# A graph-attention kernel with a new opening order, the elu minimum on another engine, and statistics combined in halves

## The chip, the core and the metric

The kernel runs on one NeuronCore of one Trainium2 chip. The core has five engines that run side by side, each with its own queue of instructions that it takes strictly in order: TensorE (PE in the profile, with its weight loads shown as PEld), VectorE (DVE), ScalarE (ACT), GpSimd (POOL) and SyncE (SP, which here only starts transfers). An instruction waits until the semaphores it names have been raised by other engines or by transfers; while it waits, everything behind it on the same engine waits too. The metric is the device time of one execution in microseconds. Before the change it is 2589.18 us, the median of three runs (2588.01 to 2589.99).

## The reference, cut to what matters

The input `x` has 16 graphs of 1024 nodes with 256 features; `adj` is one 1024 x 1024 adjacency matrix for all of them. Four layers follow each other. Each normalises, takes the positive part, runs a graph attention and adds the result to `x`:

```
h = maximum(layernorm(x), 0)
q = h @ W                                  # 256 -> 256, as H heads of D = 256 / H
e[i, j] = leaky(a_src . q[i] + a_dst . q[j])
w = softmax over j of e, only where adj[i, j] is set
x = x + elu(w @ q)                         # the last layer has relu in place of elu
```

Layers 0 and 2 have four heads of 64 columns, layers 1 and 3 one head of 256. All arithmetic is fp32.

## The kernel before, in words

**Steps.** A step is one layer of one graph, so there are 16 x 4 = 64 steps. `order_of_steps` interleaves four graphs (four "streams"), so that one-head and four-head steps alternate: the heads of the 64 steps run 4 4 4 1 4 1 1 4 1 4 1 ... 4 1 4 1 4 4 1 1 1. The two stretches in which four-head steps follow each other are the very beginning and shortly before the end.

**One step.** It has a preparation, a stretch of attention weights with aggregation, and a finish.
- Preparation (`preparation`, a list of 21 pieces). `stats` (DVE, L234) makes the layer norm's batch statistics of 4 of the 8 row blocks at a time; `combine` and `combine_end` (L257 to L269) turn them into a scale and a shift per row, in ten small instructions on GpSimd, for all eight blocks at once. `normalise` (ACT, L275) applies them, four instructions for each half of the rows; `transpose` (PE, L283) turns the half, eight instructions, and ACT moves the result out of PSUM with the positive part (L284). `project` multiplies by W (PE, L294), ACT moves each of eight results out (L296), and GpSimd scales them (L306). `factors`, `rows` and `fetch` send one attention factor per node through DRAM to all partitions.
- Weights (`weights`, DVE, L347): one instruction makes the 128 x 1024 attention weights of one head and one block of source nodes. A four-head step has 32 of them, a one-head step 8. They live in a pool of 18 buffers (`WBUFS`).
- Aggregation (`aggregate`, PE, L363): 8 groups of matmuls a step; ACT moves each group's result out of PSUM (L378). PSUM has four buffers for this ("bank") that transposes, projections and aggregations share.
- Finish (`finish`): divide by the softmax's sum (L395, and L405 on GpSimd), elu as `max(exp(min(y, 0)) - 1, y)`, and the addition to `x` (L418 on GpSimd). The minimum is on DVE in four-head steps (L404, done together with the division) and on GpSimd in one-head steps (L407); the exponential is on ACT (L411), the rest of elu on DVE (L417).

**The order of the work.** It is written out by the kernel's own planner, not by a scheduler. The main loop runs over the steps and their 8 groups; after group k of step n it emits the pieces of finish due at k and the pieces of preparations due at 8n + k (`agenda_of`, from tables such as `ONE` for one-head and `FOUR` for four-head steps: the entries are in groups, counted from two steps ahead). Then it emits the next weights, as far as buffers allow. So each engine's queue is fixed when the program is built.

**The opening.** Ahead of the loop the 8 blocks of the adjacency matrix are loaded, reduced to 0 or 1 on DVE (`sign`, L190), turned on PE (`turn`, L204), and stored as two masks, one by DVE (`positive`, L207) and one by ACT (`nonzero`, L211). Layer 0's weight columns are made (`columns`), and step 0 is prepared. Step 1 is prepared after that, step 2's statistics are emitted after step 0's first 8 weights, and the graphs of streams 2 and 3 are loaded (`load(i)`, L566) only once step 1 is prepared.

Of the kernel before, what the change touches and what calls it, by code (L numbers as in the profile page):

```python
# [38 lines left out]
STREAMS = 4  # L39
# [4 lines left out]

FOUR = (-8, -8, -5, -3, -2, -1, -1, 0, 0, 0, 0, 0, 0, 2, 2, 2, 2, 3, 8, 8, 10)
SHORT = (-4, -4, -4, -2, -2, -1, -1, 0, 0, 0, 0, 0, 0, 2, 2, 2, 2, 3, 8, 8, 10)
ONE = (2, 2, 2, 4, 4, 5, 5, 6, 6, 6, 6, 6, 6, 8, 8, 8, 8, 8, 10, 10, 12)
SOON = (0, 0, 0, 1, 2, 3, 3, 4, 4, 5, 5, 5, 5, 6, 6, 7, 7, 8, 9, 9, 11)  # L50
FIRST = (-2, -2, -2, -1, -1, -1, -1, -1, -1, -1, -1, -1, -1, -1, -1, -1, -1, -1, -1, -1, 3)
LATE = (0, 0, 0, 1, 1, 2, 2, 3, 3, 3, 3, 3, 3, 4, 4, 4, 4, 5, 6, 6, 8)


# [9 lines left out]
def kernel(ctx: ExitStack, tc: tile.TileContext, x, adj, ws, avs, out):  # L64
    nc = tc.nc
    B, N, F = x.shape
    C = N // P
# [61 lines left out]
    def weight_columns(l):  # L129

        H, slope, hs, _ = LAYERS[l]
        D = F // H
        st = {}

        def vectors(queue=nc.sync):

            st["a"] = prep.tile([P, HALF, H, D], F32, name="e")
            queue.dma_start(
                out=st["a"][0:1, 2:4],
                in_=bass.AP(tensor=avs[l].tensor, offset=avs[l].offset,  # L140
                            ap=[[0, 1], [D, 2], [hs, H], [1, D]]))

        def spread():
            pa = bank(2, H, D)
            nc.tensor.matmul(pa.rearrange("p t h d -> p (t h d)"), lhsT=ones[0:1, :],
                             rhs=st["a"][0:1, 2:4].rearrange("p t h d -> p (t h d)"),
                             start=True, stop=True)
            nc.scalar.activation(st["a"][:, 0:2], pa, AF.Copy)

        def columns():  # L150
            for k in range(K):
                for part in range(2):
                    prod = st["a"][:, 2 + part]
                    wk = heads_of(wx[l], H)[:, k]
                    nc.vector.tensor_mul(prod, wk[:, :, 0:D], st["a"][:, part])
                    nc.vector.tensor_reduce(
                        wk[:, :, D] if part else wx[l][:, k, F + H:F + 2 * H], prod, AX.X, ALU.add)
            st["sq"] = small.tile([P, K, H], F32, name="sq", bufs=1)
            wd = heads_of(wx[l], H)[:, :, :, D]
            nc.vector.tensor_tensor(st["sq"], wd, wd, op=ALU.mult)  # L160

        def bound():

            pn = bank(H)
            for k in range(K):
                nc.tensor.matmul(pn, lhsT=ones, rhs=st["sq"][:, k, :], start=(k == 0),
                                 stop=(k == K - 1))
            top = small.tile([P, 1], F32, name="top", bufs=1)
            nc.vector.tensor_reduce(top, pn, AX.X, ALU.max)
            nc.gpsimd.tensor_tensor(top, top, half1, op=ALU.pow)  # L170
            nc.gpsimd.tensor_scalar(cbias[l], top, 16.01, None, op0=ALU.mult)
            nc.gpsimd.tensor_scalar(nbias[l], top, -16.01 * slope, None, op0=ALU.mult)
            nc.gpsimd.tensor_scalar(rbias[l], top, -16.01 * (1.0 - slope), SHIFT,
                                    op0=ALU.mult, op1=ALU.add)

        return vectors, spread, columns, bound
# [45 lines left out]
    def preparation(n):  # L222
# [6 lines left out]
        def stats(half):  # L229
            if half == 0:  # L230
                st["bn"] = small.tile([P, C, 6], F32, name="bn")
            bn = st["bn"]
            for c in range(half * HALF, (half + 1) * HALF):
                nc.vector.bn_stats(bn[:, c, :], xs[b][:, c, :])  # L234
            if n == 0:
                q = slice(half * HALF, (half + 1) * HALF)
                if half == 1:
                    combine_end(slice(0, HALF), nc.vector)
                combine(q, nc.vector)
                if half == 1:  # L240
                    combine_end(q, nc.vector)

        def combine_all():
            if n > 0:
                combine(slice(0, C), nc.gpsimd)
                combine_end(slice(0, C), nc.gpsimd)

# [18 lines left out]
        def combine_end(q, engine):  # L266
            rstd, shift = (st[i][:, q] for i in ("rstd", "shift"))
            engine.tensor_tensor(shift, shift, rstd, op=ALU.mult)
            engine.tensor_scalar(shift, shift, -0.5, None, op0=ALU.mult)  # L269
# [110 lines left out]
    def finish(n):  # L380

        b, l = steps[n]
        H = LAYERS[l][0]
        D = F // H
        st = state[n]

        def views(half):
            s = slice(half * HALF, (half + 1) * HALF)
            return (xs[b][:, s, :].rearrange("p c (h d) -> p (c h) d", h=H),
                    st["y"][:, s, :, 0:D].rearrange("p c h d -> p (c h) d"),  # L390
                    st["r"][:, s, :].rearrange("p c h -> p (c h)"))

        def divide():
            st["r"] = small.tile([P, C, H], F32, name="r")
            nc.vector.reciprocal(st["r"], st["y"][:, :, :, D])  # L395

        def scaled(half):
            xh, yh, r = views(half)
            rb = r[:, :, None].to_broadcast([P, HALF * H, D])
            if l < L - 1:  # L400

                e = st["e", half] = prep.tile([P, HALF * H, D], F32, name="e")
                if H > 1:
                    nc.vector.scalar_tensor_tensor(e, yh, 0.0, rb, op0=ALU.min, op1=ALU.mult)  # L404
            nc.gpsimd.tensor_tensor(yh, yh, rb, op=ALU.mult)  # L405
            if l < L - 1 and H == 1:
                nc.gpsimd.tensor_scalar(e, yh, 0.0, -3.0e38, op0=ALU.min, op1=ALU.max)  # L407

        def exponential(half):
            if l < L - 1:  # L410
                nc.scalar.activation(st["e", half], st["e", half], AF.Exp)  # L411

        def add(half):
            xh, yh, r = views(half)
            if l < L - 1:
                e = st["e", half]
                nc.vector.scalar_tensor_tensor(e, e, -1.0, yh, op0=ALU.add, op1=ALU.max)  # L417
                nc.gpsimd.tensor_add(xh, xh, e)  # L418
                return
            nc.vector.scalar_tensor_tensor(xh, yh, 0.0, xh, op0=ALU.max, op1=ALU.add)  # L420

        def store(half):
            nc.sync.dma_start(
                out=out[b].rearrange("(p c) f -> p c f", p=P)[:, half * HALF:(half + 1) * HALF],
                in_=xs[b][:, half * HALF:(half + 1) * HALF, :])
            if half == 1 and b + STREAMS < B:
                load(b + STREAMS)


        at = (0, 0, 0, 0, 1, 1, 1) if H > 1 else (0, 0, 1, 1, 2, 2, 3)  # L430
        return list(zip(at, (divide, lambda: scaled(0), lambda: scaled(1), lambda: exponential(0),
                             lambda: exponential(1), lambda: add(0), lambda: add(1)))) + (
                    [(4, lambda: store(0)), (4, lambda: store(1))] if l == L - 1 else [])
# [60 lines left out]
    for n, (b, l) in enumerate(steps):  # L494

        free = 8 * (last[b % STREAMS] + 1) + (8 if l == 0 else 2) if b % STREAMS in last else -99
        last[b % STREAMS] = n
        start = 8 * (n - 2)
        kind = ONE if LAYERS[l][0] == 1 else SOON if n < 5 else FOUR
        if kind is FOUR and free > start + kind[0]:  # L500
            kind = SHORT
        if free > start + kind[0]:
# [10 lines left out]
    with tc.manual_schedule():  # L513
# [6 lines left out]
            blocks[c][0]()  # L520
        load(1)
        load_weights(1)
        nc.scalar.activation(warm, half1, AF.Exp)
        nc.vector.tensor_copy(identb, ident)
        layer[0][1]()
        first = [piece for _, piece in preparation(0)]

        def sign(c):

            if c < C:  # L530
                blocks[c][1]()
                blocks[c][2]()
            if c > 0:
                blocks[c - 1][3]()

        for i in (0, 1, 3, 4):
            first[i]()
        layer[0][2]()
        first[5]()
        first[6]()  # L540
        layer[0][3]()
        sign(0)
        for i, c in ((7, 1), (9, 2), (11, 3), (13, 4), (15, 5)):
            first[i]()
            first[i + 1]()
            sign(c)
        for piece in first[17:]:
            piece()
        for c in (4, 5, 0, 1, 2, 3):
            blocks[c][4]()  # L550
        done["prepared"] = 1
        plan(1)
        planned = 2
        prepare(-2)
        sign(6)
        sign(7)
        sign(8)
        emit_tiles(C, must=True)
        for _ in range(2):
            agenda.pop(0)[2]()  # L560
        blocks[6][4]()
        blocks[7][4]()
        prepare(-1)
        for i in range(2, STREAMS):
            load_weights(i)
            load(i)  # L566

        for l, at in ((1, 1), (2, 8 * 3 + 3), (3, 8 * 5 + 3)):
            for i, piece in zip((0, 1, 2, 8), layer[l]):
# [57 lines left out]
```

## Time and profile before

| what | number |
|---|---|
| time, median of three | 2589.18 us |
| span of the profiled execution | 2586.6 us |
| PE busy | 2508.0 us, 97% |
| DVE busy | 2024.0 us, 78% |
| ACT busy | 1129.3 us, 44% |
| GpSimd busy | 1034.3 us, 40% |
| mean granted TensorE clock | 0.992 |

The page also has the span cut into 40 slices of 64.7 us: PE is at 60% in the first, 80% in the second and 90% or more after that. A busy PE is not a PE at its peak: 256 aggregating matmul records of a four-head step take 7.69 us when nothing holds them up, and count as busy for longer when they arrive one weight buffer at a time. So the page's shares say where to look, and the timeline of a stretch says what ends each wait.

### The profile page before, as it was taken

What the parts mean: (1) busy time and instruction counts of PE and PEld (TensorE: products, weight loads), DVE (VectorE), ACT (ScalarE), POOL (GpSimd) and SP (SyncE); (2) the same over time, 40 slices, a digit from 0 to 9 for tenths busy, and PEclk for the clock granted to TensorE, in tenths of its full rate; (3) what the DMA queues carried; (4) which work ended last, traced back from release to release, by engine and by line L of the source; (5) the groups of instructions that cost most, each with busy time, mean ns of one, the idle gap of its engine ahead of it and who ended that gap; (6) DMA issues with size and microseconds to landing.
All of it is one profiled execution on the core that took longest, in us unless ns stands there. A gap on an engine that the chain in (4) does not pass through costs nothing.

```text
span 2586.6 us, 87821 instructions
## 1 busy us (share of the span) xinstructions
PE 2508.0 (97%) x40088; PEld 2257.8 (87%) x40088; DVE 2024.0 (78%) x2144; ACT 1129.3 (44%) x2502; POOL 1034.3 (40%) x1040
## 2 busy tenths in 40 slices
PE   6889999999999999999999999999999999999999
PEld 4788888899888899888899888998888998889888
DVE  5997678877778877778877778877778877787973
ACT  5344444434444444544344544344444345444341
POOL 2143444432443444543323444543433345444331
PEclk8899999999999999999999999999999999999999
DMA  3210011111112100102211111101112201111101
GB/s 142 73 44 35 18 34 43 43 60 59 59 51 76 43 27 27 43 35 75 76 53 66 43 35 43 43 19 68 50 59 76 76 11 43 35 43 43 52 18 57
DMA packets 36987, 128.98 MB, mean 50 GB/s; under 512 B 6278, under 2 KB 9094, under 8 KB 34696
## 3 DMA queue, kind: packets, MB, share of 16 engines
q1 hardware_dynamic: 36606, 123.36, 13.6%
q8 instruction: 314, 5.14, 0.8%
q14 instruction: 57, 0.47, 0.1%
q10 hardware_dynamic: 10, 0.00, 0.0%
HBM read 105.91 MB, written 17.43 MB: 48 GB/s over the span
## 4 chain that ended last, share of the span: by engine, by line
PE 57%; DVE 26%; POOL 9%; issue 5%; ACT 3%; DMA 1%; DVEq 0%; SPq 0%; ACTq 0%
PE bank L363 36%; DVE w L347 17%; PE bank L294 17%; POOL x L418 5%; PE bank L283 4%; DVE bn L234 3%; DVE e L417 2%; ACT xn L275 2%; DVE e L404 2%; POOL rstd L263 2%; DMA x<-in_x 0%; ACT e L411 0%; PE bank L318 0%; DVE r L395 0%; POOL shift L269 0%
## 5 line engine op out<-in xcount | busy, mean ns | idle before, releaser
L363 PE MATMUL bank<-whx,w 128*64 128x65 f32 x36864 | 1904.8, 241 | 32.6 <-DVE w L347 20.8
L363 PEld LDWEIGHTS bank<-whx,w 128*64 128x64 f32 x36864 | 1742.1, 144 | 176.5 <-DVE w L347 25.5
L347 DVE SCALAR_TENSOR_TENSOR w<-g,rcol,mask 128x1024 f32<-128x1024 f32 x1280 | 1540.4, 1273 | 378.0 <-PE bank L363 337.3
L378 ACT ACTIVATE y<-bank 128x260 f32<-128x260 f32 (+1 forms) x504 | 194.4, 386 | 1093.4 <-PE bank L363 1093.4
L306 POOL TENSOR_TENSOR whx<-whx 128x1024 f32<-128x1024 f32 x128 | 258.5, 2020 | 666.0 <-ACT whx L304 666.0
L405 POOL TENSOR_TENSOR y<-y,r 128x1024 f32<-128x1024 f32 x126 | 264.4, 2108 | 582.1 <-DVE e L404 454.9
L294 PE MATMUL bank<-wx,hT 128*128 128x264 f32 (+1 forms) x2048 | 476.5, 387 | 3.7 <-ACT hT L284 3.7
L294 PEld LDWEIGHTS bank<-wx,hT 128*128 128x128 f32 x2048 | 384.6, 191 | 66.3 <-ACT hT L284 4.6
L418 POOL TENSOR_TENSOR x<-x,e 128x1024 f32<-128x1024 f32 x96 | 248.0, 2593 | 135.7 <-DVE e L417 135.7
L275 ACT ACTIVATE xn<-x,shift,rstd 128x256 f32<-128x256 f32 x512 | 261.2, 590 | 82.9 <-POOL shift L269 80.8
L296 ACT ACTIVATE whx<-bank 128x264 f32<-128x264 f32 (+1 forms) x512 | 194.9, 386 | 208.1 <-PE bank L294 207.7
L234 DVE BATCH_NORM_STATS2 bn<-x 128x6 f32<-128x256 f32 x512 | 175.9, 412 | 97.2 <-POOL x L418 74.0
L417 DVE SCALAR_TENSOR_TENSOR e<-e,y 128x1024 f32<-128x1024 f32 x96 | 158.0, 1663 | 34.2 <-ACT e L411 26.9
L283 PE MATMUL bank<-ident,xn 128*128 128x128 f32 x1024 | 155.2, 281 | 22.9 <-ACT xn L275 22.4
L283 PEld LDWEIGHTS bank<-ident,xn 128*128 128x128 f32 x1024 | 120.4, 141 | 59.6 <-ACT xn L275 48.5
L342 ACT ACTIVATE g<-gs 128x1024 f32<-128x1024 f32 x160 | 163.6, 1022 | 11.1 <-DVE w L347 8.4
L284 ACT ACTIVATE hT<-bank 128x512 f32<-128x512 f32 x256 | 136.6, 585 | 0.3 <-PE bank L283 0.2
L263 POOL TENSOR_TENSOR rstd<-rstd,neghalf 128x8 f32<-128x8 f32 (+1 forms) x65 | 107.0, 1646 | 12.5 <-DVE shift L264 7.6
L411 ACT ACTIVATE e<-e 128x1024 f32<-128x1024 f32 x96 | 100.7, 1049 | 12.7 <-DVE e L404 12.7
L404 DVE SCALAR_TENSOR_TENSOR e<-y,r 128x1024 f32<-128x1024 f32 x64 | 75.6, 1222 | 2.5 <-DVE r L395 0.5
L420 DVE SCALAR_TENSOR_TENSOR x<-y,x 128x1024 f32<-128x1024 f32 x30 | 43.4, 1445 | 10.0 <-POOL y L405 10.0
L257 POOL TENSOR_TENSOR dev<-bn 128x8 f32<-128x8 f32 x63 | 14.6, 231 | 87.4 <-DVE bn L234 87.4
(63 smaller groups left out, 401.7 us busy)
## 6 DMA issues: line engine op xcount, KB each, us to landing
gs<-grow SPq DMA_DIRECT2D x160, 512.0 KB
x<-in_x SPq DMA_DIRECT2D x15, 1024.0 KB
out<-x SPq DMA_DIRECT2D x30, 512.0 KB
w<-in_adj SPq DMA_DIRECT2D x8, 512.0 KB
x<-in_x SPq DMA_DIRECT2D x2, 512.0 KB
wx<-in_L_gnn_W SPq DMA_DIRECT2D x8, 128.0 KB
out<-x SPq DMA_DIRECT2D x8, 128.0 KB
grow<-gT SPq DMA_DIRECT2D x32, 16.0 KB
```

The lines of the kernel that those rows point to most:

```text
L234: nc.vector.bn_stats(bn[:, c, :], xs[b][:, c, :])
L275: nc.scalar.activation(xn[:, q, :], xs[b][:, c, :], AF.Identity, bias=st["shift"][:, c:c + 1], scale=st["rstd"][:, c:c + 1])
L283: nc.tensor.transpose(pt[:, q, :], st["xn", half][:, q, k * P:(k + 1) * P], ident)
L294: nc.tensor.matmul(pw, lhsT=st["hT", half][:, k, q * P:(q + 1) * P], rhs=wx[l][:, k, :], start=(k == 0), stop=(k == K - 1))
L296: nc.scalar.activation(st["whx"][:, c, :], pw, AF.Copy)
L306: nc.gpsimd.tensor_tensor(wh[:, :, :, 0:D], wh[:, :, :, 0:D], wh[:, :, :, D:D + 1].to_broadcast([P, HALF, H, D]), op=ALU.mult)
L347: nc.vector.scalar_tensor_tensor(w, state[n]["g", h], state[n]["rcol"][:, jc, h:h + 1], masks[LAYERS[steps[n][1]][3]][:, jc, :], op0=ALU.m ...
L363: nc.tensor.matmul(acc[o % P:o % P + cols, q, :], lhsT=st["w", h, jc][:, o:o + cols], rhs=st["whx"][:, jc, h * (D + 1):(h + 1) * (D + 1)], ...
L378: nc.scalar.activation(st["y"][:, i0:i0 + per, h, :], acc, AF.Copy)
L405: nc.gpsimd.tensor_tensor(yh, yh, rb, op=ALU.mult)
L417: nc.vector.scalar_tensor_tensor(e, e, -1.0, yh, op0=ALU.add, op1=ALU.max)
L418: nc.gpsimd.tensor_add(xh, xh, e)
```

## The change

There are four edits.
1. **The opening** is written as one explicit list. Streams 2 and 3 (`load(2)`, `load(3)`) are loaded at the start, behind the adjacency matrix. Step 1's statistics move between the masks (`prepare(-4)`), and its two halves are normalised, turned and projected among step 0's first groups of aggregation instead of ahead of them (the new table `FIRST`). The two masks are made block by block as the turns arrive. Step 3's preparation is due one group later.
2. **The elu minimum** is placed by the step that runs beside it: on DVE where the next step has one head, on GpSimd where the next has four. Of the 64 steps this changes four: steps 0, 1 and 59 (from DVE to GpSimd) and step 5 (from GpSimd to DVE).
3. **Statistics in two parts**: in one-head steps the ten small GpSimd instructions run for each half of the row blocks, behind that half's statistics, instead of once for all eight blocks. Each half is normalised with its own result. Four-head steps keep the single combination.
4. **The last two steps** get a table of their own (`TIGHT`), which puts their preparations three groups later up to the transposes, and one to two groups later at the end.

The diff, without the lines that only move blank space:

```diff
-FIRST = (-2, -2, -2, -1, -1, -1, -1, -1, -1, -1, -1, -1, -1, -1, -1, -1, -1, -1, -1, -1, 3)
+FIRST = (-4, -4, -4, -2, 0, -1, -1, -1, -1, -1, -1, 1, 1, 2, 2, 2, 2, 2, 3, 3, 5)
+TIGHT = (5, 5, 5, 7, 7, 8, 8, 9, 9, 9, 9, 9, 9, 10, 10, 10, 10, 10, 11, 11, 13)
...
-        def columns():
-            for k in range(K):
+        def columns(ks=range(K)):
+            for k in ks:
...
+            q = slice(half * HALF, (half + 1) * HALF)
             if n == 0:
-                q = slice(half * HALF, (half + 1) * HALF)
                 if half == 1:
                     combine_end(slice(0, HALF), nc.vector)
                 combine(q, nc.vector)
-                if half == 1:
-                    combine_end(q, nc.vector)
+            elif H == 1:
+                combine(q, nc.gpsimd)
+                combine_end(q, nc.gpsimd)

         def combine_all():
-            if n > 0:
+            if n == 0:
+                combine_end(slice(HALF, C), nc.vector)
+            elif H > 1:
                 combine(slice(0, C), nc.gpsimd)
                 combine_end(slice(0, C), nc.gpsimd)
...
         def scaled(half):
+            time = LAYERS[steps[n + 1][1]][0] == 1
             if l < L - 1:
                 e = st["e", half] = prep.tile([P, HALF * H, D], F32, name="e")
-                if H > 1:
+                if time:
                     nc.vector.scalar_tensor_tensor(e, yh, 0.0, rb, op0=ALU.min, op1=ALU.mult)
             nc.gpsimd.tensor_tensor(yh, yh, rb, op=ALU.mult)
-            if l < L - 1 and H == 1:
+            if l < L - 1 and not time:
                 nc.gpsimd.tensor_scalar(e, yh, 0.0, -3.0e38, op0=ALU.min, op1=ALU.max)
...
-        start = 8 * (n - 2)
-        kind = ONE if LAYERS[l][0] == 1 else SOON if n < 5 else FOUR
+        start = 8 * (n - 2) + (n == 3)
+        kind = (ONE if n < len(steps) - 2 else TIGHT) if LAYERS[l][0] == 1 else SOON if n < 5 else FOUR
...
         load(1)
         load_weights(1)
+        for i in range(2, STREAMS):
+            load(i)
...
+        order = (
+            [first[0], first[1], first[3], lambda: layer[0][2](range(1)), first[2],
+             lambda: layer[0][2](range(1, K)), first[5], first[6], first[4], layer[0][3]]
+            + [blocks[c][1] for c in range(4)]
+            + [first[7], first[8], blocks[0][2], blocks[4][1], blocks[5][1], blocks[0][3],
+               first[9], first[10], blocks[1][2], blocks[0][4], blocks[6][1], blocks[7][1],
+               blocks[1][3], first[11], first[12], blocks[2][2], blocks[1][4],
+               lambda: prepare(-4), first[13], first[14], blocks[3][2], blocks[2][4],
+               blocks[2][3], blocks[3][3], first[15], first[16]]
+            + [first[17], blocks[4][2], blocks[5][2], first[18], first[19],
+               blocks[4][3], blocks[3][4], blocks[4][4], blocks[5][3], blocks[5][4],
+               blocks[6][2], blocks[7][2], blocks[6][3], blocks[6][4], blocks[7][3], blocks[7][4]])
         plan(1)
         planned = 2
+        for piece in order:
+            piece()
+        done["prepared"] = 1
+        emit_tiles(C // 2, must=True)
         prepare(-2)
-        sign(6)
-        sign(7)
-        sign(8)
         emit_tiles(C, must=True)
-        for _ in range(2):
-            agenda.pop(0)[2]()
-        blocks[6][4]()
-        blocks[7][4]()
         prepare(-1)
         for i in range(2, STREAMS):
             load_weights(i)
-            load(i)
```

More of the change, by code (lines that the diff above doesn't have):

```diff
@@ L157, in columns @@
                         wk[:, :, D] if part else wx[l][:, k, F + H:F + 2 * H], prod, AX.X, ALU.add)
+            if K - 1 not in ks:
+                return
             st["sq"] = small.tile([P, K, H], F32, name="sq", bufs=1)
@@ L526 @@
         first = [piece for _, piece in preparation(0)]
[L528 to L551, printed above, removed]
+        order = (
[10 more added lines that the diff above has]
+               blocks[6][2], blocks[7][2], blocks[6][3], blocks[6][4], blocks[7][3], blocks[7][4]])
         plan(1)
         planned = 2
+        for piece in order:
+            piece()
+        done["prepared"] = 1
+        emit_tiles(C // 2, must=True)
         prepare(-2)
-        sign(6)
-        sign(7)
-        sign(8)
         emit_tiles(C, must=True)
-        for _ in range(2):
-            agenda.pop(0)[2]()
-        blocks[6][4]()
-        blocks[7][4]()
         prepare(-1)
```

## The prediction

> **What bounds the kernel now.** I read the page's engine shares first, then the slices, then the waits, and last the timelines of the opening, of one step in the middle, and of the end.
>
> ```profile
> PE 2508.0 (97%) x40088; PEld 2257.8 (87%) x40088; DVE 2024.0 (78%) x2144; ACT 1129.3 (44%) x2502; POOL 1034.3 (40%) x1040
> ...
> PE   6889999999999999999999999999999999999999
> PEld 4788888899888899888899888998888998889888
> DVE  5997678877778877778877778877778877787973
> ```
>
> TensorE is the engine to keep fed. The first two slices (129 us) are the only ones in which it is plainly not, and there DVE is half idle in slice one and full in slices two and three. So the kernel has two regimes: an opening bound by DVE up to about 200 us, and then TensorE. What TensorE or DVE waits for:
>
> ```profile
> DVE bn L234 <- DMA x<-in_x: 23.3, 2, 20.0
> ...
> PE bank L283 <- ACT xn L275: 22.4, 87, 3.8
> ```
>
> The first line is one wait of 20.0 us on a load of `x`; the second is 87 small waits of the transposes for normalised rows, some 15 us of them outside the opening. They are the two places I price.
>
> ```profile
> 39.53 9.63 DVE L347 SCALAR_TENSOR_TENSOR w<-g,rcol,mask 128x1024 f32<-128x1024 f32 x8 [0.79 <-ACT g L342]
> 69.13 2.71 DVE L234 BATCH_NORM_STATS2 bn<-x 128x6 f32<-128x256 f32 x8 [19.98 <-DMA x<-in_x]
> 71.76 21.52 DVE L347 SCALAR_TENSOR_TENSOR w<-g,rcol,mask 128x1024 f32<-128x1024 f32 x18
> ```
>
> In the opening DVE makes 8 weights, then sits in front of step 2's statistics, whose graph was asked for only at 63.71 us and landed at 69 us. All later weights are queued behind. From 71.76 to 200 us DVE never idles for over 1 us.
>
> ```profile
> 888.54 5.58 POOL L418 TENSOR_TENSOR x<-x,e 128x1024 f32<-128x1024 f32 x2 [1.16 <-DVE e L417]
> ...
> 895.64 0.21 POOL L257 TENSOR_TENSOR dev<-bn 128x8 f32<-128x8 f32 x1 [1.52 <-DVE bn L234]
> ...
> 899.59 0.24 POOL L269 TENSOR_SCALAR shift<-shift 128x8 f32<-128x8 f32 x1
> ...
> 899.86 4.04 ACT L275 ACTIVATE xn<-x,shift,rstd 128x256 f32<-128x256 f32 x8 [2.26 <-POOL shift L269]
> ...
> 900.51 0.33 PE L283 MATMUL bank<-ident,xn 128*128 128x128 f32 x1
> 901.00 0.33 PE L283 MATMUL bank<-ident,xn 128*128 128x128 f32 x1 [0.16 <-ACT xn L275]
> ...
> 902.59 3.64 PE L363 MATMUL bank<-whx,w 128*128 128x257 f32 x16
> ```
>
> This is step 20, a one-head step in the middle. The ten small GpSimd instructions end at 899.83, ACT starts normalising at once, and the transposes follow ACT at one normalised block per 0.49 us. The eight transposes hold PE from 900.51 to 902.59, 2.08 us; unhindered they take 0.97 us (1381.79 to the next group at 1382.76). The loss is 1.1 us, more than the 0.49 us shown as idle, because the busy time is stretched too.
>
> **The Trainium skill.** "Perfetto Trace Analysis", section "Optimizing Scalar/DVE Operations", says that where ScalarE and VectorE aren't saturated but cause bubbles elsewhere, breaking up instructions may let work complete sooner: that is edit 3, and the trace agrees on the bubbles (GpSimd is 40% busy). The same section warns that moving work between DVE and GpSimd might not help, since they share an SBUF read port. "SBUF — State Buffer" names DVE instructions with two SBUF inputs as those that contend with GpSimd's reads. Here L417, which has two, takes 1.22 us alone and 1.66 us in the mean, 2.9 us at worst beside GpSimd, which agrees. "DMA: Bandwidth & Descriptors", section "Bandwidth", has 341 GB/s for a 1 MB load; the opening here moved 397 to 415 GB/s from 10 to 20 us.
>
> **Opening.** The two early loads (2 MB) at the 415 GB/s seen take 5.1 us. Transfers are idle from about 20 to 34 us, so they land by 26 us, hidden beside the mask work, ahead of the broadcasts. The first weight should stay near 39.5 us: the list holds the same 8 signs, 8 positives and 8 statistics on DVE, and the chain through step 0's projections to the broadcast of its factors is not shorter by more than a microsecond. Then 8 weights (9.6 us) and 8 statistics (2.7 us) end at 51.9 us, so DVE reaches weight 9 at 51.9 instead of 71.76: **19.9 us** earlier. TensorE must keep up. It starts aggregating near 48 instead of 60.35 us. From 60.35 us to the end of step 2 (209.81) it now does 3 steps of 1024 records at 7.69 us per 256 (92.3), three preparations of some 10 (30) and 2.5 of odds, 125 us in 149; the change adds half of step 1's preparation (5), so the earliest end is 48 + 130 = 178 us, and 20 us is within reach but tight. Following both queues, DVE would fill its 18 buffers once, some 4 us before TensorE ends step 0 at about 100 us: minus 4. The minimum: step 1 saves two L404 (2.4 us) and waits 0.2 to 0.8 us longer for the exponential. In step 0 only two weights lie between division and L417, and GpSimd's chain per half is 2.0 (L405) + 1.04 (L407) with 1.05 on ACT, ready at 4.1 and 7.2 us: two waits of 1.7 us take back the 2.4 saved. Behind that exponential on ACT are the moves out of PSUM, for which PE already waits 2.96 us at 172.7; that grows by 1.8 us where DVE is the bound anyway. Sum **19.9 - 4 + 2 = 18 us**; bounds 8 (TensorE binds earlier) and 22. From step 3 on both kernels are TensorE-bound, so it is kept.
>
> **Statistics in halves.** In the changed kernel's instruction order, everything from step 7 to 57 is the same on PE, DVE and ACT; only GpSimd differs. For all eight blocks the ten instructions take 4.19 us (895.64 to 899.83). No row shows nine of them at four blocks on GpSimd; the tenth, the power, takes 1.03 at four blocks in step 0 against 1.67. Bounds for a half: 3.5 us (the others as long as now, which their 0.29 us spacing suggests) and 4.2. I take 3.5. Half 0 can start when L418 ends, at 894.12, and is ready at 897.6, when ACT has just moved out a group (897.22 + 0.39). Four normalisations take 2.07: done at 899.7, before PE arrives at 900.5. The transposes then take 0.97: 1.1 us saved. Half 1 is ready at 901.1 (now 899.83), normalised at 903.2; ACT behind it moves out the waiting group and the transposes (0.3 + 1.06): 904.6. PE wants them at 901.4 + 3.5 = 904.9, so the new wait just fits, by 0.3 us. With 4.2 a half, half 1 comes at 902.5, ACT ends at 906.0, and a new wait of 1.1 us eats the gain. Of the 25 one-head steps from 8 to 56, 16 show 0.41 to 0.49 us of idle (1.1 lost), 8 show 0.71 to 0.81 (1.45 lost, by the same count at 1446.50), one 0.16 (0.4): 17.6 + 11.6 + 0.4 = 29.6 us. As the margin of 0.3 us won't hold always I take off 0.2 a step: **24 us**; bounds 0 and 30.
>
> **End.** Steps 59 and 60 are DVE-bound; the last weight of step 60 is done at 2474.8 and PE has no gap after it. The moved minimum of step 59 brings that some 1.4 us forward. The later preparation of step 62 moves 1 us of transposes behind it, and step 63's weights come one group (3.5 us) later, ending near 2558.7 where its first group would be done at 2558.2: 1 us. Sum 0, bounds -3 and +3. Step 5's minimum and step 3's shift lie beside TensorE-bound work: 0.
>
> **Forecast and rivals.**
> - Forecast, 0.62: 2589 - 18 - 24 = 2547 us.
> - The second half comes late and takes the whole gain of the halves (0.17): 2589 - 18 = 2571. For it: margin 0.3 us, GpSimd's unmeasured small instructions. Against: their spacing doesn't follow size.
> - TensorE binds the opening, which gives 8 (0.13): 2589 - 8 - 24 = 2557. For it: 130 us of its work in that stretch; against: it idles 13 us between 60 and 81 us, before DVE has caught up.
> - Slower (0.06): GpSimd's extra 2.8 us also delays the next four-head step's combination (now done at 903.92, wanted by ACT at 905.02), ACT stands in front of its moves, PE runs out of banks and loses 1.6 us in 25 steps, 40 us: 2589 - 18 + 40 = 2611. Against: that combination would end at 905.1, 0.1 late.
> - No change needs both gains to cancel: 0.02.
>
> Faster is the sum of the first three, 0.92. The range runs from all bounds at their best (2589 - 22 - 30 - 3 = 2534, and two for rounding), to the second rival and some microseconds (2574).
>
> **What would show it.** The wait of DVE on `x` of 20.0 us is gone and weight 9 starts near 52 us; step 2 ends near 192 us. In the middle the transposes' wait for normalised rows falls from 22.4 us to some 5, and a pair of steps takes 76.7 instead of 77.6 us. I am wrong if PE waits for the moved-out transposes (L284) in every one-head step, or if step 2 ends after 200 us.

## The result, and the profile after

The changed kernel takes 2560.54 us (median of four, 2558.53 to 2563.94), against 2588.6 us before: ratio 0.9894, 95% interval 0.9877 to 0.9911. It gains 28 us where 42 were forecast. Lines moved down by about eight: the weights are now L355, the aggregation L371, the move out of PSUM behind it L386, the transposes L291, normalising L283.

The page of the changed kernel, engine shares and slices:

```profile
PE 2497.2 (98%) x40088; PEld 2258.7 (88%) x40088; DVE 2018.9 (79%) x2140; ACT 1130.0 (44%) x2502; POOL 1110.1 (43%) x1364
...
PE   6899999999999999999999999999999999999899
...
DVE  8888578888778888778888778888778878778863
```

Slice three of PE went from 8 to 9 (before, three slices were below 90%, and not only the two that the texts above name), but slice 38, near the end, fell from 9 to 8. DVE is fuller in slice one (8 for 5). GpSimd has 324 more instructions and 76 us more busy time. Its waits (what waits, for what: us in total, times, longest):

```profile
DVE w L355 <- ACT g L350: 77.8, 9, 22.2
...
PE bank L291 <- ACT xn L283: 10.3, 4, 6.9
...
PE bank L371 <- ACT whx L304: 7.5, 2, 4.8
...
PE bank L326 <- ACT gcol L321: 7.1, 2, 6.3
...
PE bank L302 <- ACT y L386: 4.4, 9, 0.5
...
DVE bn L238 <- DMA x<-in_x: 3.3, 1, 3.3
```

The two waits that were priced are gone: DVE's 20.0 us on `x` (the 3.3 us left were there before, at the start), and the transposes' waits outside the opening, 0.4 us where there were 15.5; the other 9.9 of the 10.3 us lie in the opening. In their place stand waits that no sum had: one of 6.3 us of PE on ACT's `gcol` (L321, the factors that `rows` sends out), one of 4.8 us on ACT's move of a projection (L304; 2.96 us before), nine of 0.5 us on ACT's move of an aggregation (L386), and DVE's wait for `g` (the factors broadcast to all partitions), which went from 40.8 to 77.8 us, 37.5 of them for the weights of the last two steps.

The move out of PSUM of a step's eighth group (L386, on ACT) marks the end of that step, and in the last step, which has no such move, DVE's last reciprocal of a result does (L380). Differences between these marks in the trace divide the span into stages:

| stage (us) | before | after | gain | forecast |
|---|---|---|---|---|
| start to the end of step 2 | 209.81 | 199.42 | 10.4 | 18 |
| steps 3 to 7 | 201.6 | 201.6 | 0 | 0 |
| steps 8 to 58 | 1985.98 | 1962.25 | 23.7 | 24 |
| steps 59 to 63 | 185.09 | 192.37 | -7.3 | 0 |

Together 26.8 us, the difference of the two spans (2586.6 and 2559.7). The same kernel profiled a second time, as an experiment below, gives 196.93 for the opening, 1962.72 for the middle and 192.28 for the end. So the middle came as forecast, the opening brought 10 to 13 us of 18, and the end lost time where the sum had zero.

**The middle.** The same step 20 that the prediction read, now in the changed kernel (start and length in us):

```profile
878.04 0.19 POOL L265 TENSOR_TENSOR dev<-bn 128x4 f32<-128x4 f32 x1
...
881.32 0.23 POOL L277 TENSOR_SCALAR shift<-shift 128x4 f32<-128x4 f32 x1
...
881.59 2.08 ACT L283 ACTIVATE xn<-x,shift,rstd 128x256 f32<-128x256 f32 x4
...
884.55 1.03 PE L291 MATMUL bank<-ident,xn 128*128 128x128 f32 x8
884.79 0.23 POOL L277 TENSOR_SCALAR shift<-shift 128x4 f32<-128x4 f32 x1
...
885.05 2.07 ACT L283 ACTIVATE xn<-x,shift,rstd 128x256 f32<-128x256 f32 x4 [1.39 <-POOL shift L277]
...
887.30 1.06 ACT L292 ACTIVATE hT<-bank 128x512 f32<-128x512 f32 x2
```

A half takes 3.51 us on GpSimd (878.04 to 881.55), the 3.5 that the prediction took. Half 0 is normalised 0.9 us before the transposes begin, and they take 1.03 us without a break instead of 2.08. Half 1 is ready at 885.02; the moves behind it end at 888.36, and PE begins the projection that needs them at 888.90, with no wait: a margin of 0.5 us. Most one-head steps take 33.63 or 34.10 us where they took 34.56 or 35.02. The nine new waits of 0.5 us lie in steps of 34.10 us. At 660.54 us, for instance, GpSimd has combined the next four-head step's statistics 1.3 us later in the step than before, ACT normalises for that step first, from 658.14 to 660.21 us, and only then moves an aggregation out (L386, 660.12 us), for which PE's projection waits 0.49 us.

### The profile page after: what moved, and what is told of

Read it like the earlier page. It is cut to its first block, busy times and chain, and to the rows that moved or that the text cites. A ratio compares the mean times of both kernels' runs of the same rounds, so it can differ in the third digit from the quotient of the medians.

```text
span 2559.7 us, 88174 instructions
## 1 busy us (share of the span) xinstructions
PE 2497.2 (98%) x40088; PEld 2258.7 (88%) x40088; DVE 2018.9 (79%) x2140; ACT 1130.0 (44%) x2502; POOL 1110.1 (43%) x1364
## 3 DMA queue, kind: packets, MB, share of 16 engines
q1 hardware_dynamic: 36606, 123.36, 13.7%
## 4 chain that ended last, share of the span: by engine, by line
PE 84%; DVE 9%; POOL 3%; issue 2%; ACT 2%; DMA 0%; DVEq 0%; POOLq 0%; ACTq 0%
PE bank L371 63%; PE bank L302 17%; DVE w L355 7%; PE bank L291 4%; DVE bn L238 1%; ACT xn L283 1%; POOL x L427 1%; POOL rstd L271 1%; DVE e L426 0%; PE bank L326 0%; POOL y L414 0%; DVE e L413 0%; POOL e L416 0%; ACT g L350 0%; DMA x<-in_x 0%
## 5 line engine op out<-in xcount | busy, mean ns | idle before, releaser
L371 PE MATMUL bank<-whx,w 128*64 128x65 f32 x36864 | 1909.5, 241 | 29.3 <-DVE w L355 17.6
L371 PEld LDWEIGHTS bank<-whx,w 128*64 128x64 f32 x36864 | 1745.1, 145 | 174.3 <-DVE w L355 24.3
L355 DVE SCALAR_TENSOR_TENSOR w<-g,rcol,mask 128x1024 f32<-128x1024 f32 x1280 | 1540.2, 1272 | 392.1 <-PE bank L371 314.3
L386 ACT ACTIVATE y<-bank 128x260 f32<-128x260 f32 (+1 forms) x504 | 193.9, 385 | 1090.9 <-PE bank L371 1090.9
L302 PE MATMUL bank<-wx,hT 128*128 128x264 f32 (+1 forms) x2048 | 482.2, 388 | 5.6 <-ACT y L386 4.4
L283 ACT ACTIVATE xn<-x,shift,rstd 128x256 f32<-128x256 f32 x512 | 264.6, 590 | 73.2 <-POOL shift L277 71.2
L304 ACT ACTIVATE whx<-bank 128x264 f32<-128x264 f32 (+1 forms) x512 | 188.7, 384 | 178.3 <-PE bank L302 177.8
L291 PE MATMUL bank<-ident,xn 128*128 128x128 f32 x1024 | 137.9, 277 | 10.5 <-ACT xn L283 10.3
L291 PEld LDWEIGHTS bank<-ident,xn 128*128 128x128 f32 x1024 | 120.8, 142 | 27.7 <-ACT xn L283 14.6
L271 POOL TENSOR_TENSOR rstd<-rstd,neghalf 128x4 f32<-128x4 f32 (+1 forms) x97 | 120.2, 1239 | 15.1 <-DVE shift L272 7.6
L420 ACT ACTIVATE e<-e 128x1024 f32<-128x1024 f32 x96 | 100.7, 1049 | 23.4 <-POOL e L416 23.1
L312 ACT ACTIVATE whx<-whx,nbias 128x16 f32<-128x16 f32 (+1 forms) x128 | 40.2, 314 | 4.2
```

The costliest lines, as they stand in the source:

```text
L283: nc.scalar.activation(xn[:, q, :], xs[b][:, c, :], AF.Identity, bias=st["shift"][:, c:c + 1], scale=st["rstd"][:, c:c + 1])
L291: nc.tensor.transpose(pt[:, q, :], st["xn", half][:, q, k * P:(k + 1) * P], ident)
L302: nc.tensor.matmul(pw, lhsT=st["hT", half][:, k, q * P:(q + 1) * P], rhs=wx[l][:, k, :], start=(k == 0), stop=(k == K - 1))
L304: nc.scalar.activation(st["whx"][:, c, :], pw, AF.Copy)
L355: nc.vector.scalar_tensor_tensor(w, state[n]["g", h], state[n]["rcol"][:, jc, h:h + 1], masks[LAYERS[steps[n][1]][3]][:, jc, :], op0=ALU.m ...
L371: nc.tensor.matmul(acc[o % P:o % P + cols, q, :], lhsT=st["w", h, jc][:, o:o + cols], rhs=st["whx"][:, jc, h * (D + 1):(h + 1) * (D + 1)], ...
```

## The experiments

Twelve kernels, each profiled and timed against the kernel before. Stage times are read as above. Since the opening of one kernel differs between profiles by up to 2.5 us, openings are compared as means over kernels with the same opening where there are several. The end differs by as much: it is the same in experiments 5, 7, 9, 10 and 12, and takes 186.31 to 188.70 us there.

**1. The minimum back on DVE in every four-head step.**

```diff
-            time = LAYERS[steps[n + 1][1]][0] == 1
+            time = H > 1
```

> The changed kernel with one edit undone: the elu minimum is on DVE in all four-head steps again. Theory A (the minimum on GpSimd is a cost: ACT stands longer in front of the exponential, with the moves out of PSUM behind it): in step 0's finish the 6.3 us for which PE waits for the factors' transpose falls to 4 us or less, DVE's two waits there (1.9 and 2.0 us) and the one of 5.4 us in step 59's finish go, together some 4 to 6 us: 2555 to 2557. Rival B (the minimum is hidden, TensorE binds there anyway): the time stays within 1 us of 2560.5. Rival C (all of the loss at the end is the minimum's): 7 us at the end alone, below 2554.

Measured: 2557.16 us, ratio 0.9866 (0.9851 to 0.9881), an interval that overlaps that of the changed kernel. The opening ends at 195.98 us and the last five steps take 190.30. PE's wait for the factors' transpose fell to 4.68 us, less than expected. What the minimum does at the end is seen in step 59 of the changed kernel:

```profile
2411.09 0.34 DVE L403 RECIPROCAL r<-y 128x32 f32<-128x32 f32 x1
...
2411.51 1.90 POOL L414 TENSOR_TENSOR y<-y,r 128x1024 f32<-128x1024 f32 x1 [9.46 <-DVE r L403]
2413.50 1.04 POOL L416 TENSOR_SCALAR e<-y 128x1024 f32<-128x1024 f32 x1
...
2414.57 1.06 ACT L420 ACTIVATE e<-e 128x1024 f32<-128x1024 f32 x1 [6.66 <-POOL e L416]
2415.53 1.19 ACT L304 ACTIVATE whx<-bank 128x258 f32<-128x258 f32 x4
...
2415.95 9.22 PE L371 MATMUL bank<-whx,w 128*64 128x65 f32 x256 [4.80 <-ACT whx L304]
...
2421.78 1.05 ACT L420 ACTIVATE e<-e 128x1024 f32<-128x1024 f32 x1
...
2422.86 1.22 DVE L426 SCALAR_TENSOR_TENSOR e<-e,y 128x1024 f32<-128x1024 f32 x1 [5.37 <-ACT e L420]
```

and in the same step of the kernel before:

```profile
2445.20 0.34 DVE L395 RECIPROCAL r<-y 128x32 f32<-128x32 f32 x1
...
2446.84 1.06 ACT L411 ACTIVATE e<-e 128x1024 f32<-128x1024 f32 x1 [4.82 <-DVE e L404]
...
2448.22 7.69 PE L363 MATMUL bank<-whx,w 128*64 128x65 f32 x256 [2.96 <-ACT whx L296]
...
2453.66 1.82 DVE L417 SCALAR_TENSOR_TENSOR e<-e,y 128x1024 f32<-128x1024 f32 x1 [1.02 <-ACT e L411]
```

From the reciprocal to the first exponential it is 1.64 us before and 3.48 after. The moves out of PSUM (L304) stand behind the exponential on ACT, so PE waits 4.80 us instead of 2.96. The next group then ends later, its move (L386) stands in front of the second exponential, and DVE waits 5.37 us for that instead of 1.02. About 1.5 us of this come from a fall of TensorE's clock behind the wait (256 records in 9.22 us instead of 7.69), which experiment 12 takes up. DVE is the engine that is short here: two minima saved on it cost it more in waiting.

**2. Without the later table for the last two steps.**

```diff
-        kind = (ONE if n < len(steps) - 2 else TIGHT) if LAYERS[l][0] == 1 else SOON if n < 5 else FOUR
+        kind = ONE if LAYERS[l][0] == 1 else SOON if n < 5 else FOUR
```

> The changed kernel with one edit undone: the last two steps use the table of the other one-head steps. After step 58 the changed kernel takes 192.4 us to the last group against 185.1 before. Theory A (the later preparation took TensorE work out of a stretch in which it waits for weights, and brought the last weights late): 5 to 7 us of the 7.3 come back, 2554 to 2556. Rival (the minimum of step 59 is the cause): the time stays within 1.5 us of 2560.5.

Measured: 2560.31 us, ratio 0.9881 (0.9866 to 0.9896). There is no difference in time that can be told, so 5 to 7 us did not come back. But in the trace steps 61 to 63 take 36.82, 31.40 and 27.80 us as before, instead of 40.80, 37.96 and 29.14, while step 60 takes 53.63 instead of 43.96. The end is 190.16, 2.2 us less. Weights of the last steps in the changed kernel:

```profile
2482.93 9.62 DVE L355 SCALAR_TENSOR_TENSOR w<-g,rcol,mask 128x1024 f32<-128x1024 f32 x8 [15.27 <-ACT g L350]
2491.41 0.30 PEld L371 LDWEIGHTS bank<-whx,w 128*128 128x128 f32 x2 [0.71 <-DVE w L355]
...
2520.89 9.63 DVE L355 SCALAR_TENSOR_TENSOR w<-g,rcol,mask 128x1024 f32<-128x1024 f32 x8 [22.19 <-ACT g L350]
2529.38 0.30 PEld L371 LDWEIGHTS bank<-whx,w 128*128 128x128 f32 x2 [0.71 <-DVE w L355]
```

DVE waits 15.27 and 22.19 us for the factors, as these steps are prepared so late, and PE's weight loads then wait for the last weights as they come (0.71 us before the seventh); PE itself waits 0.8 us for them in each of the last two steps, and not at all without the table. Before, step 62's preparation stood in step 60, where PE has gaps of 7.0 us in its trace (3.0 for the move of a projection, 2.9 for weights, 1.1 for normalised rows); now it stands in step 61, which had no gap to fill. What each of the two, late weights and lost gaps, has of the 2.2 us is not shown.

**3. Statistics whole, as before, the rest as changed.**

```diff
-            elif H == 1:
-                combine(q, nc.gpsimd)
-                combine_end(q, nc.gpsimd)
...
-            elif H > 1:
+            else:
```

> The changed kernel with one edit undone: the statistics of one-head steps are combined for all eight blocks at once again. Theory A (the halves are what shortens the middle): the one-head steps of the middle take 34.56 or 35.02 us again instead of 33.6 or 34.1, 24 us in all: 2584. Rival (the middle is shorter because the opening shifted the engines against each other): 2560 to 2567.

Measured: 2584.37 us, ratio 0.9973 (0.9961 to 0.9984). The middle takes 1987.84 us and PE waits 24.0 us for normalised rows in 83 waits. So the whole gain of the middle is that of the halves, as the prediction had it.

**4. The kernel before with the two early loads, nothing else.**

```diff
         load(1)
         load_weights(1)
+        for i in range(2, STREAMS):
+            load(i)
...
         for i in range(2, STREAMS):
             load_weights(i)
-            load(i)
```

> The kernel before with one part of the change: the graphs of streams 2 and 3 are loaded behind the adjacency matrix. Theory A (the load was the whole of the opening's wait on DVE, and what follows is bound by TensorE's queue and by ACT): DVE's wait of 20.0 us goes, weight 9 starts near 52 us, step 2 ends 10 to 16 us earlier than 209.8, and the time is 2573 to 2579. Rival B (without the new order TensorE, which starts its aggregation at 60.4 us, binds at once): step 2 ends within 5 us of 209.8, 2584 or more. Rival C (the order adds nothing): as much as DVE gains, 2569.

Measured: 2574.81 us, ratio 0.9938 (0.9923 to 0.9952). Step 2 ends at 196.09 us, 13.7 earlier than before: as much as with the whole new order of pieces (199.42 and 196.93). In step 0 the new order is ahead (96.66 us against 101.97), and by step 1 that is gone (148.36 against 148.66). So the two moved lines bring the opening's gain, and something in the changed kernel takes back what its order adds.

**5. Minimum on DVE, and no later table.** Edits 1 and 2 together.

> The changed kernel with two edits undone: the minimum on DVE in all four-head steps, and no table of its own for the last two steps. After step 58 the changed kernel takes 192.4 us to the last group, the one with the minimum undone 190.3, the one with the table undone 190.2, and the kernel before 185.1. Theory A (each of the two alone costs 5 us, and together they overlap): 185 to 186 us here, and a time of 2549 to 2553. Rival (something else of the changed kernel, such as the halves, costs 3 us or more at the end): 188 us or more.

Measured: 2552.71 us, ratio 0.9856 (0.9841 to 0.9871); the end takes 187.42 us. That is between the two expectations. With experiments 1 and 2, it splits the end's loss: 2.7 us the minimum (190.16 - 187.42), 2.2 the table (192.37 - 190.16), and 2.3 that remain (187.42 - 185.09). Undone in the other order it is 2.1 for the minimum and 2.9 for the table. These are differences of single profiles, so they hold to a microsecond or two.

**6. As changed, with step 1's counts taken two groups earlier.**

```diff
-FIRST = (-4, -4, -4, -2, 0, -1, -1, -1, -1, -1, -1, 1, 1, 2, 2, 2, 2, 2, 3, 3, 5)
+FIRST = (-4, -4, -4, -2, 0, -1, -1, -1, -1, -1, -1, 1, 1, 2, 2, 2, 2, 2, 3, 3, 3)
```

The last entry says after which of step 0's groups step 1 counts as prepared and its weights may be issued.

> The changed kernel with one number changed: step 1 counts as prepared after group 3 of step 0 instead of group 5 (the last entry of the table for step 1), so that DVE's first weights of step 1 stand earlier. Theory A (the 6.2 us for which DVE waits for step 1's first factors delay the division of step 0, and ACT and TensorE behind it): that wait falls to 2 us or less, TensorE's wait for the factors' transpose from 6.3 to 2 us or less, and step 2 ends 3 to 6 us earlier, near 195; 2555 to 2558. Rival (TensorE binds this stretch, DVE's wait is slack): step 2 ends within 1.5 us of 199.

Measured: 2556.43 us, ratio 0.9872 (0.9858 to 0.9887); step 1 ends at 140.58 us and step 2 at 194.16. DVE's wait for `g` is gone (1.06 us for a free buffer is left) and PE's wait for the factors' transpose is 1.43 us, as the first theory has it. The changed kernel's opening shows why, and how the minimum adds to it:

```profile
37.96 9.62 DVE L355 SCALAR_TENSOR_TENSOR w<-g,rcol,mask 128x1024 f32<-128x1024 f32 x8 [3.26 <-ACT g L350]
47.51 2.70 DVE L238 BATCH_NORM_STATS2 bn<-x 128x6 f32<-128x256 f32 x8
50.13 11.99 DVE L355 SCALAR_TENSOR_TENSOR w<-g,rcol,mask 128x1024 f32<-128x1024 f32 x10
...
89.06 19.16 DVE L355 SCALAR_TENSOR_TENSOR w<-g,rcol,mask 128x1024 f32<-128x1024 f32 x16 [6.19 <-ACT g L350]
...
108.14 0.34 DVE L403 RECIPROCAL r<-y 128x32 f32<-128x32 f32 x1
...
108.56 1.90 POOL L414 TENSOR_TENSOR y<-y,r 128x1024 f32<-128x1024 f32 x1 [5.54 <-DVE r L403]
110.55 1.04 POOL L416 TENSOR_SCALAR e<-y 128x1024 f32<-128x1024 f32 x1
...
111.63 1.06 ACT L420 ACTIVATE e<-e 128x1024 f32<-128x1024 f32 x1 [8.48 <-POOL e L416]
...
112.93 0.32 ACT L321 ACTIVATE gcol<-gcol,shift 128x32 f32<-128x32 f32 x1
...
113.30 0.39 PE L326 MATMUL bank<-ident,gcol 128*32 128x128 f32 x1 [6.31 <-ACT gcol L321]
```

DVE reaches weight 9 at 50.13 us, as forecast. But it then waits 6.19 us for step 1's first `g`, and the 16 weights behind that keep the reciprocal of step 0 back until 108.14 us, 11.5 us after step 0's last move out of PSUM (96.66). GpSimd divides and takes the minimum, 2.94 us of work, ACT waits 8.48 us for it, and everything behind ACT waits too: the `gcol` of the next preparation, and so PE, 6.31 us.

**7. The kernel before with early loads and statistics in halves.** Experiment 4 with the changed kernel's halves added; the old order of the opening, the old minimum and the old table stay.

> The kernel before with two parts of the change alone: the early loads, and the statistics in halves. Theory A (these two carry the whole gain; the new order, the moved minimum and the table for the last steps add nothing or cost): 14 us in the opening and 24 in the middle, 2549 to 2553, faster than the changed kernel by 8 us. Rival (the new order is worth what it was written for): 2560 or more.

Measured: 2553.61 us, ratio 0.9859 (0.9844 to 0.9874); opening 195.21, middle 1964.87, end 186.31. These two edits do better than the whole change (experiment 8, on the same chip: 2559.11 to 2563.66 against 2551.84 to 2553.84).

**8. The changed kernel again**, beside runs 5 to 7 on their chip.

> The changed kernel once more, on the chip of the three others, as the measure for them: 2558 to 2563 if the differences of a few us between kernels are to mean anything; step 2 ends between 197 and 200 us, the last group comes 192 to 193 us after step 58.

Measured: 2559.48 us, ratio 0.9888 (0.9872 to 0.9905); opening 196.93. Means of the opening: 197.9 us over the four kernels that have the changed one (199.42, 196.95, 198.44, 196.93), and 195.1 over the two with the minimum on DVE (195.98, 194.31). By this the minimum costs the opening some 2.8 us, from few profiles; their spread is taken up under "What stays open".

**9. All three undone**: edits 1, 2 and 6 together.

> The changed kernel with the minimum back on DVE in all four-head steps, without the later table for the last two steps, and with step 1's first counts prepared at group 3 instead of group 5. Theory (each of the three undoes a separate wait): step 2 ends near 191 to 194 us, the middle stays at 1964, the end takes 187 to 188 as with the first two alone; 2547 to 2550 us, the fastest so far. Rival (the opening's loss is half-clock stretches that any order meets): step 2 ends at 194 to 196 and the time is 2552 to 2554, no better than without the third edit.

Measured: 2548.93 us (2545.3 to 2549.56), ratio 0.9837 (0.9823 to 0.985). Step 2 ends at 189.18 us, earlier than expected; the middle takes 1965.65 and the end 187.43. The same stretch of the opening:

```profile
102.52 0.34 DVE L403 RECIPROCAL r<-y 128x32 f32<-128x32 f32 x1
102.90 2.36 DVE L413 SCALAR_TENSOR_TENSOR e<-y,r 128x1024 f32<-128x1024 f32 x2
104.16 1.06 ACT L420 ACTIVATE e<-e 128x1024 f32<-128x1024 f32 x1 [1.72 <-DVE e L413]
...
105.46 0.32 ACT L321 ACTIVATE gcol<-gcol,shift 128x32 f32<-128x32 f32 x1
...
106.12 0.27 PE L326 MATMUL bank<-ident,gcol 128*32 128x128 f32 x1
```

The reciprocal comes 5.6 us earlier, the exponential 7.5 us earlier, and PE does not wait for `gcol` here at all.

**10. The same, with step 3's preparation due as before.**

```diff
-        start = 8 * (n - 2) + (n == 3)
+        start = 8 * (n - 2)
```

> The kernel of the three undone costs, with step 3's preparation due as before, one group earlier. Theory (the shift lies beside TensorE-bound work): within 2 us of that kernel, step 2's end and steps 3 to 7 the same. Rival (the shift keeps step 3's statistics out of DVE's way in step 1): step 2 ends 2 to 4 us later.

Measured: 2547.65 us, ratio 0.9839 (0.9826 to 0.9853); step 2 ends at 189.62 us and steps 3 to 7 take 201.52. The shift does nothing that can be seen there. The end, which this edit does not touch, takes 188.70 us here, 1.3 more than in experiment 9.

**11. As 9, with statistics whole in the last three steps.**

```diff
-            elif H == 1:
+            elif H == 1 and n < len(steps) - 4:
...
-            elif H > 1:
+            elif H > 1 or n >= len(steps) - 4:
```

> The kernel of the three undone costs, with statistics combined whole in the last three steps and in halves elsewhere. Theory (the halves cost at the end, where a second chain of GpSimd instructions stands between a pre-empted normalisation and its moves): the end takes 185 to 186 us instead of 187 to 188, about 2 us less in all. Rival (the 1.2 us seen at the end beside halves is a half-clock stretch that falls where it likes): the end is unchanged at 187 to 188.

Measured: 2547.01 us, ratio 0.9836 (0.9822 to 0.9849), not to be told from experiment 9; in the trace the end takes 185.10 us, as expected of the first theory, but the next run shows another reason for the 2.3 us.

**12. The kernel before with the halves only.** The edit of experiment 3 turned round, on the kernel before.

> The kernel before with the statistics of one-head steps in halves and nothing else. Theory (gains of opening and middle add up): the middle, from the end of step 7 to the end of step 58, falls from 1986 to 1962 to 1965 us; opening 210, end 185 to 186.5; about 2566 us. Rival (part of the middle's gain needs the earlier opening): 2570 or more.

Measured: 2570.86 us, ratio 0.9927 (0.9915 to 0.994). That is in the rival's range, but not for its reason: the middle takes 1963.68 us, its full gain of 22.3 without the opening. What I had left out are losses elsewhere, 0.7 us in the opening (210.5) and 2.3 at the end (187.42): 22.3 - 3.0 = 19.3, and 2589.74 - 19.3 = 2570.4.

The 2.3 us can be followed here. Of the aggregation behind the wait in step 60, this kernel's timeline, and then its engines in two windows (busy us and records of PE, PEld, DVE, ACT, POOL; then the granted TensorE clock):

```profile
2426.78 9.26 PE L366 MATMUL bank<-whx,w 128*64 128x65 f32 x256 [2.96 <-ACT whx L299]
...
2433.80 2.57 DVE L420 SCALAR_TENSOR_TENSOR e<-e,y 128x1024 f32<-128x1024 f32 x1 [2.60 <-ACT e L414]
```

```profile
2426.80:2430.20 3.40, 3.40 (x70) 3.40 (x72) 3.40 (x3) 1.86 (x7) 3.40 (x3) 0.57 0.03 7
2430.20:2432.40 2.20, 2.20 (x74) 2.20 (x72) 1.00 (x1) 0.04 (x1) 2.20 (x1) 0.89 0.00 0
```

The same window of the kernel before:

```profile
2448.30:2451.70 3.40, 3.40 (x118) 3.40 (x120) 3.40 (x3) 1.80 (x7) 3.40 (x3) 1.00 0.02 5
```

The wait is 2.96 us in both, and from the last two groups of step 59 up to it the two run alike. After it, the granted clock is 0.57 in the first window here and 1.00 there: 70 records in 3.40 us against 118. The 256 records take 9.26 us instead of 7.69, 1.57 more, and DVE's wait for the second exponential grows by 1.58 (1.02 to 2.60). The shifted L420 then overlaps an addition on GpSimd and takes 2.57 us instead of 1.82, 0.75 more. Together 2.33, without any new wait for a half. Why the clock fell here and not there is taken up in the last section.

## Why the prediction was right, and where not

- **Opening, 19.9 us (weight 9).** Right: 50.13 us against 71.76 is 21.6, and the early loads are hidden. The surplus is the first weight, at 37.96 us where the sum had kept 39.53.
- **Minus 4 us, DVE fills its buffers once.** Too large: step 0 ends 18.4 us earlier, and with the three edits undone step 2 ends at 189.2 to 191.0 us, 18.8 to 20.6 earlier. DVE's wait for a free buffer is 1.1 us in experiments 6, 9 and 10, and the changed kernel has none in the opening. TensorE does not bind the opening at 8 us, which rules out the third case of the forecast.
- **Plus 2 us for the minimum.** Wrong in sign. The 2 us were to be saved in step 1; for step 0 I set two waits of 1.7 us against 2.4 us saved, and the waits did come (1.94 and 2.02 us), but put what stands behind the exponential on ACT at nothing, as DVE was the bound. It costs 2.8 us in the mean; among the profiles with equally many half-clock stretches it is 1.8 ("What stays open" has them).
- **Missing from the sum: step 1 counts as prepared two groups late.** The new table's last entry, 5 for 3, makes DVE wait 6.19 us for `g`. I had read the table as moving preparation only. Taking it back alone gives 3.8 us (197.9 to 194.16); with the minimum 8.0 (197.9 to 189.9, the mean of experiments 9 to 11). Both end in the same wait of PE, which may be why together they give a little more than 2.8 + 3.8. The opening's term of 18 us, of which 10 to 13 came, was mis-sized by these two.
- **Statistics in halves, 24 us.** Right with its mechanism: 23.7 us, 3.51 us a half, transposes of 1.03 us. The second case of the forecast (half 1 late) did not come. The sum is closer than its parts: the one-head steps gain 22.2 us, most of them 0.92 each, also those that were priced at 1.45, and the rest lies in a few four-head steps. The 0.2 us a step taken off for a failing margin was spent elsewhere: the margin held, but the wait that the "Slower" case feared came in small, 0.5 us in nine steps instead of 1.6 in 25. The sentence of the Trainium skill on breaking up instructions, which the prediction cites, speaks of ScalarE and VectorE; here the same held for GpSimd.
- **End, 0 us.** This step failed, at -7.3 us. It said that the moved minimum brings step 60's last weight 1.4 us forward and that the later preparation moves "1 us of transposes" behind it. The first counted DVE's busy time and not what DVE then waits for: the traces of experiment 1 show a loop of DVE, GpSimd, ACT, PE and ACT, and the experiments its price, 2.1 to 2.7 us. The second saw the preparation as a cost wherever it stands; in step 60 PE had pauses, and the move out of it, with the late weights that came of it, cost 2.2 to 2.9 us. The remaining 2.3 us are, as far as experiment 12 shows, no term of the change: there they are a stretch of half clock behind an old wait, which the profile of the kernel before happened to escape.
- **Step 5's minimum and step 3's shift, 0.** Right: steps 3 to 7 take 201.6 us in both, and experiment 10 changed nothing.

**What stays open.** The five profiles with halves, but without the moved minimum and the table, lost 1.2 to 3.6 us at the end; the three whose last steps have none of these (before, experiments 4 and 11) lost none. The last section shows that half clock depends on where a wait falls on a grid that the kernel does not set, so this may be chance, but eight profiles do not prove it. For the same reason the shares of the minimum and the table are rough. The spread of the opening goes with the clock as well: up to the end of step 2 the four profiles of the changed opening have 10, 8, 7 and 7 half-clock windows of 3.4 us and end at 199.42, 198.44, 196.95 and 196.93 us. The two with the minimum on DVE have 7 each (195.98 and 194.31). That these windows are the whole cause of the spread is not shown.

## What to carry to other kernels

Price a moved instruction by the queue that its consumer stands in: 1.8 us more to an exponential on ACT held up every move out of PSUM behind it, TensorE, and through TensorE the engine that was to be relieved. Work placed in a stretch where TensorE waits for another engine can be hidden there, so before moving it later, see whether the place it goes to has pauses as well. Undo the edits of a bundle one by one: here the halves and two moved loads did better alone (2553.61 us) than the whole change, and with three costs taken back the kernel took 2548.93 us instead of 2560.54, faster than both kernels.

## What the hardware did that I had not expected

A wait of TensorE of under 3 us can cost a second time: behind the 2.96 us of experiment 12 the clock fell, and where DVE waits for what TensorE makes, the 1.6 us are passed on in full. In the changed kernel the aggregation behind the wait of 4.80 us takes 9.22 us, much the same.

"TensorE: Matmul & The Clock Gate" of the Trainium skill, part 1, section "What's actually happening", has the clock at one half after an idle window of about 3.4 us, and the window as free-running. The traces agree with the length and the half: 3.4 us at half rate lose 1.70 us of clock, and the two windows of experiment 12 lose 3.40 x 0.43 + 2.20 x 0.11 = 1.70. They also agree that the window runs freely. In each of the 14 traces, all stretches of half clock begin and end on one grid of 3.413 us, to within 0.005 us. Its place differs from trace to trace, by 2.2 us between the two profiles of the changed kernel, so the kernel does not set it.

The traces do not agree that a whole window must be idle. Counting windows of this grid at full clock, without the first 20 and the last 8 us, all 63 in which TensorE was busy for less than 1.4 us were followed by half clock, and none of the 10085 in which it was busy for more than 2.05 us; between these both occur. So what counts is how much of a wait falls into one window. Of the wait of 2.96 us in step 60, one window holds 2.91 us in experiment 12 (2423.87 to 2427.28 us, and the half clock lasts from there to 2430.70) and 2.15 to 2.47 us in experiments 1, 5, 9 and 10, and half clock follows. In the kernel before and in experiments 4 and 7 the grid cuts the same wait into parts of at most 1.94 us, and it does not.

The 0.75 us of experiment 12 agrees with "SBUF — State Buffer", section "SBUF: two separate sides", by which a DVE instruction with two SBUF inputs and one of GpSimd exclude each other.
